# Own views for routed rows' stores, one table set for the first attention's roots, and an earlier first expert

## The chip, the cores and the metric

The kernel runs on one core of a Trainium2 chip. The core has five engines with a queue of instructions each: TensorE (PE, matrix products; PEld is its load of weights), VectorE (DVE), ScalarE (ACT, functions from tables, of which one set at a time is loaded), GpSimd (POOL) and SyncE (SP, which mostly issues DMAs). An engine works through its queue in order, and waits at an instruction until the semaphores that it needs are set. DMAs are issued by SP, ACT and POOL. The metric is device time in microseconds (us); lower is better.

## The reference

Two rounds of attention and of a mixture of experts (MoE) over x, 4 batches of 512 rows of 256 floats, and a context of 4 x 1601 rows of 256:

```
def _layernorm(x, axis=-1, eps=1e-05):
    m = jnp.mean(x, axis=axis, keepdims=True)
    v = jnp.var(x, axis=axis, keepdims=True)
    return (x - m) / jnp.sqrt(v + eps)
...
def _L0_xattn_ref(x, latents, ...):       # x: context, latents: layernorm of the rows
    xn = _layernorm(x, gamma_media, beta_media)
    ln = _layernorm(latents, gamma_lat, beta_lat)
    q = ln @ Wq + bq
    kv_input = jnp.concatenate([xn, ln], axis=1)
    k, v = jnp.split(kv_input @ Wkv + bkv, 2, axis=-1)
    ...
    attn = jax.nn.softmax(sim, axis=-1)   # 8 heads of 128, 512 x 2113 for each batch and head
    ...
    return out @ Wo + bo
...
x = x + _L0_xattn_ref(ctx_1024, _layernorm(x), ...)
x = x + _L0_ffn_ref(_layernorm(x), ...)   # top 2 of 8 experts, with a capacity, 256-1024-256, gelu
x = x + _L1_xattn_ref(ctx_1024, _layernorm(x), Wq, Wk, Wv, 1, 0, 1)   # 8 heads of 32, 512 x 1601
x = x + _L1_ffn_ref(_layernorm(x), ...)   # top 2 of 8 experts, softmax of the two, gelu
```

All of it is in float32.

## The kernel before

**Opening (0 to about 44 us).** For batch 0 `keys_input` (lines near L750 to L850) normalises the latents (`latents`, `latents_again`: two layer norms, one on the other), turns them with PE into `kvin`, and does the same with 13 tiles of context: `first` takes mean and variance of 4, 4 and 5 tiles with DVE's bn_stats and bn_aggr (L826, L827), the reciprocal root with `ln_scale`, and normalises on ACT (L834); `ctx_group` turns and scales. `queries_keys` makes qT and kT. All this is inside `in_order(computing)`: the engines run it in the order in which it is written, which is the list at L1024.

**Roots.** `ln_root` (L157) has two ways. While `both_tables` is set, by `logarithms(True)` (L128), it is Ln and Exp on ACT out of a table set that holds both. Otherwise it is Sqrt (L166), from another set than the attention's Exp (L958), and a reciprocal on DVE (L169). `ln_scale` adds one Newton step on DVE. `logarithms(True)` stands ahead of the second attention only.

**First attention (to about 1566 us).** A step n of the 128 is a batch b, a head h and a tile t of 128 rows. `scores` (PE, L944) fills the one buffer `ps_s`, 2113 columns; `top` (DVE, L952) takes the row maxima; `softmax` (ACT, L958) takes the exps into one of two `attn`; `exchange` (L965) sends 16 DMAs, 12 on SP and 4 on ACT, that swap blocks between partitions; `turn` (DVE, L973) ends the transpose into pT. For every two steps follow `weigh` (PE, L981), a copy oT (ACT, L1133) and `project` (PE, L992), whose result DVE adds to x (L1002). Work of the next heads and batches (queries, keys L890, values L927, moments) is laid between the steps in the list `later`, and a scheduler orders the instructions inside a step.

The main loop (L1053) runs four steps past the last, for the tail. At n == n_steps it closes the pool stack `right`, which holds what the attention needs on that side, opens the MoE's pools in its place, and calls `fetched(0, 0)` (L630: SP's loads of an expert's rows sx and weights w1, w2) and `turned` (L641: four transposes tp_x on PE, a copy sxT on DVE, L647). One step later comes `hidden` (L652: PE L657 and Gelu on ACT, L664), whose Gelus are kept in program order.

**First MoE (about 1566 to 1856 us).** Eight experts in two halves each: `fetched`, `turned`, `hidden` and the second layer (L1348, ps_y). Rows were scattered to experts' slots by POOL.

**Second attention (about 1856 to 2412 us).** 112 units of work and a tail of five, by a schedule that is written out (`place`, `put`), in order on PE, DVE and ACT. At a batch's end, on PE the result is turned (L1626), DVE divides it (`got`, L1636), and POOL adds it to x (L1643). Then `route2(b)` of that batch runs within the next batch's steps: layer norm, router, places of each row in its experts' lists, and `scatters` (L588): POOL's indirect DMAs store a row's 265 floats (`pay`: the normalised row and its number) in two DRAM tensors. For batches 0 to 2 that are eight scatters into `rows_a` (the experts' first tiles) and eight into `rows_b` (what overflows), for batch 3 eight into `rows_b`. They come out in pairs, between the other steps. Each scatter names the whole of `rows_a` or `rows_b` as its target (L594), so that the framework's tracker sees a write behind a write and makes it wait for the one before.

POOL's queue around the end of the second attention is, before and after the change: eight rows_a scatters of batch 2, an x-add (L1643), eight rows_b scatters, the last x-add (L1643), then the second MoE's stores. On DVE the layer norm of batch 3's last rows (L144, L145) and behind it the copy of the first expert's xT (L1487) follow that last x-add. SP's queue has `cw<-rows_a` (L1683, `load_first_rows`: the first expert's rows), then the loads of the next experts' rows (L1835) and weights (L1843).

**Second MoE (about 2404 to 2707 us).** `first_layer` (L1690) and `first_tile`: PE turns the rows (L1486), first layer (L1495), second (L1872); DVE scales y (L1899), POOL adds it to the output in DRAM by an indirect DMA (L1885). Overflowing rows are gathered from `rows_b` by POOL (L2009).

Of the kernel before, what the change touches and what calls it, by code (L numbers as in the profile page):

```python
# [7 lines left out]

F32 = mybir.dt.float32
# [66 lines left out]
def rows_of(i, n, tail):  # L76
    return tail if i == n - 1 else P
# [6 lines left out]
def xattn_ffn_twice(ctx: ExitStack, tc: tile.TileContext, a: dict, out: bass.AP):  # L84
# [355 lines left out]
    def route2(b, two, psum, tag, first=0, n=NT):  # L440
# [146 lines left out]
        def scatters():  # L587

            sent = 0
            for rows, at in ((rows_a, place_a), (rows_b, place_b))[b == B - 1 :]:  # L590
                for k in range(2):
                    for t in range(n):
                        j = b * NT + first + t
                        nc.gpsimd.indirect_dma_start(  # L594
                            out=rows[:, :],
                            out_offset=bass.IndirectOffsetOnAxis(ap=at[k][:, j : j + 1], axis=0),
                            in_=pay[:, t, :],
                            in_offset=None,
                            bounds_check=E * G - 1 if rows is rows_a else ROWS - 1,
                            oob_is_err=False,  # L600
                        )
                        sent += 1
                        if sent % 2 == 0:
                            yield
# [16 lines left out]
        yield from sending  # L621


    banks, tags = {}, {}

    def slots(of, e, half, n=CT):
# [46 lines left out]
    with ExitStack() as st:  # L673
# [72 lines left out]
        def keys_input(b, ctx_b):  # L746
# [68 lines left out]
            def ctx_group(n0):  # L815
                group(ctx_b, n0, min(4, NM - n0), S + n0 * P, gbm, TAIL, NM)

            def first(n0, n):
# [12 lines left out]
                for i in range(n):  # L831
                    r = rows_of(n0 + i, NM, TAIL)
                    of = ctx_b[:r, n0 + i, :]
                    nc.scalar.activation(  # L834
                        of, of, AF.Identity, scale=rs[:r, i : i + 1], bias=away[:r, i : i + 1]
                    )

            if b == 0:
                steps = [latents, latents_again, lambda: group(state["lat"], 0, NT, 0, gbl, P, NT)]

                groups = ((0, 4), (4, 4), (8, NM - 8))
                return steps, (
                    [lambda n0=n0, n=n: first(n0, n) for n0, n in groups],
                    [lambda n0=n0: ctx_group(n0) for n0 in range(0, NM, 4)],
                )

# [159 lines left out]
        def output_bias():  # L1006
# [8 lines left out]
            nc.vector.tensor_tensor(bo, bo, ps, ALU.add)  # L1015
            add_output_bias(0)

        opening = ExitStack()
        opening.enter_context(in_order(*computing))
        latent, context = keys_input(0, ctx_b)  # L1020
# [31 lines left out]
        early = late = ()  # L1052
        for n in range(n_steps + 4):  # L1053
            b, h, t = n // (H0 * NT), n // NT % H0, n % NT
            if n == n_steps:

                right.close()
                b_y = ctx.enter_context(tc.tile_pool(name="b_y", bufs=2, side="right"))
                b_two = ffn1.enter_context(tc.tile_pool(name="b_two", bufs=2, side="right"))
                banks.update(m=ps_t, h=ps_t)  # L1060
                tags.update(m="t", h="t")
                ahead = turned(*fetched(0, 0))
            if n == n_steps + 1:
                ahead = hidden(*ahead, behind=True)
            if n < n_steps:
                if t == 0:
# [1148 lines left out]
```

## Time and profile before

| | us |
|---|---|
| three runs | 2706.76, 2707.55, 2708.15 |
| their median | 2707.55 |
| the profiled execution | 2708.6 |
| its span, first to last instruction | 2706.9 |
| PE busy in it | 2634.4 |
| last matmul ends | 2693.2 |
| granted TensorE clock, mean over the span | 0.994 |
| one table load on ACT (35 of them) | 1.283 |
| scatters L594 into rows_a, rows_b | 24 and 32 |

Busy time is that of one profiled execution. An engine's wait is put down to the instruction that ended it. `x8` behind a row is the number of instructions that it stands for; one float32 matmul of L657, L944, L981 or L1348 shows as two of them. A granted clock of 1.00 means that TensorE's clock was let through whole.

### The profile page before, as it was taken

What the parts mean: (1) busy time and instruction counts of PE and PEld (TensorE: products, weight loads), DVE (VectorE), ACT (ScalarE), POOL (GpSimd) and SP (SyncE); (2) the same over time, 40 slices, a digit from 0 to 9 for tenths busy, and PEclk for the clock granted to TensorE, in tenths of its full rate; (3) what the DMA queues carried; (4) which work ended last, traced back from release to release, by engine and by line L of the source; (5) the groups of instructions that cost most, each with busy time, mean ns of one, the idle gap of its engine ahead of it and who ended that gap; (6) DMA issues with size and microseconds to landing.
All of it is one profiled execution on the core that took longest, in us unless ns stands there. A gap on an engine that the chain in (4) does not pass through costs nothing. (4 is left out here: it accounts for less than half of the span.)

```text
span 2706.9 us, 38439 instructions
## 1 busy us (share of the span) xinstructions
PE 2634.4 (97%) x14748; PEld 1790.0 (66%) x14748; DVE 1346.0 (50%) x2445; ACT 918.7 (34%) x1577; POOL 352.3 (13%) x372
## 2 busy tenths in 40 slices
PE   6999999999999999999999999999999999989997
PEld 3666676666666666766666678876454544458887
DVE  6544556644456544454454341124777878733111
ACT  4332234323334333333232321122444444452221
POOL 0000000100000100000100000102432431222542
PEclk9999999999999999999999999999999999999999
DMA  5444434433443433433343465553433200035673
GB/s 179 111 113 122 99 90 114 102 95 88 109 113 85 115 96 87 99 93 88 100 100 96 124 188 164 179 177 100 128 115 108 82 10 10 17 109 170 199 226 78
DMA packets 191325, 302.92 MB, mean 112 GB/s; under 512 B 41783, under 2 KB 113272, under 8 KB 188440
## 3 DMA queue, kind: packets, MB, share of 16 engines
q1 hardware_dynamic: 152392, 218.33, 28.9%
q0 software_dynamic: 14160, 46.31, 5.8%
q10 hardware_dynamic: 24576, 35.68, 5.2%
q8 instruction: 119, 1.95, 0.3%
q14 instruction: 78, 0.64, 0.1%
HBM read 111.46 MB, written 51.07 MB: 60 GB/s over the span
## 5 line engine op out<-in xcount | busy, mean ns | idle before, releaser
L952 DVE TENSOR_REDUCE top<-ps_s 128x1 f32<-128x2113 f32 x128 | 301.8, 2358 | 584.8 <-PE ps_s L944 583.6
L981 PE MATMUL ps_o<-pT,v 128*128 128x256 f32 x2176 | 519.4, 380 | 0.0
L944 PE MATMUL ps_s<-kT,qT 128*128 128x512 f32 (+1 forms) x1280 | 489.1, 526 | 5.8 <-ACT attn L958 5.8
L981 PEld LDWEIGHTS ps_o<-pT,v 128*128 128x128 f32 x2176 | 407.8, 190 | 110.6 <-issue 65.4
L958 ACT ACTIVATE attn<-ps_s,top 128x2113 f32<-128x2113 f32 x128 | 259.1, 2024 | 477.4 <-DVE top L952 457.8
L944 PEld LDWEIGHTS ps_s<-kT,qT 128*128 128x128 f32 x1280 | 241.8, 190 | 251.7 <-issue 235.8
L973 DVE STREAM_TRANSPOSE pT<-swapped 128x2176 f32<-128x2176 f32 x128 | 312.4, 2440 | 31.2 <-DMA swapped<-attn 22.5
L1295 DVE TENSOR_REDUCE tops<-ps_s 128x1 f32<-128x512 f32 (+2 forms) x428 | 251.5, 648 | 129.1 <-PE ps_s L1284 128.0
L890 PE MATMUL ps_k<-kvin,wkv 128*128 128x512 f32 (+2 forms) x640 | 259.4, 528 | 3.4 <-DVE kvin L810 3.0
L927 PE MATMUL ps_v<-wkv,kvin 128*128 128x256 f32 x1088 | 255.3, 381 | 2.0 <-ACT v L934 1.4
L927 PEld LDWEIGHTS ps_v<-wkv,kvin 128*128 128x128 f32 x1088 | 204.7, 190 | 38.4 <-issue 6.0
L1565 ACT ACTIVATE pT<-ps_w 128x512 f32<-128x512 f32 (+1 forms) x384 | 184.3, 565 | 124.5 <-PE ps_w L1551 124.4
L906 ACT ACTIVATE kT<-ps_k,bqk 128x512 f32<-128x512 f32 (+1 forms) x192 | 101.0, 556 | 259.9 <-PE ps_k L890 124.0
L890 PEld LDWEIGHTS ps_k<-kvin,wkv 128*128 128x128 f32 x640 | 115.7, 191 | 75.2 <-issue 64.0
L934 ACT COPY v<-ps_v 128x512 f32<-128x512 f32 x144 | 80.2, 561 | 213.1 <-PE ps_v L927 141.1
L1284 PE MATMUL ps_s<-kv,qT 32*128 32x512 f32 (+1 forms) x1024 | 127.7, 553 | 3.4 <-DVE got L1636 3.2
L1551 PE MATMUL ps_w<-qT,kv 32*128 32x256 f32 (+1 forms) x1664 | 118.0, 383 | 0.0
L657 PE MATMUL ps_h<-sxT,w 128*128 128x256 f32 (+1 forms) x512 | 108.0, 367 | 4.0 <-DVE sxT L647 2.5
L744 POOL TENSOR_TENSOR x<-x,bo 128x256 f32<-128x256 f32 x16 | 11.7, 760 | 742.9 <-DVE lat L182 545.6
L1348 PE MATMUL ps_y<-w,hT 128*128 128x256 f32 x480 | 107.8, 380 | 0.0
L657 PEld LDWEIGHTS ps_h<-sxT,w 128*128 128x128 f32 x512 | 91.8, 190 | 21.1 <-issue 4.2
L1348 PEld LDWEIGHTS ps_y<-w,hT 128*128 128x128 f32 x480 | 90.2, 190 | 14.9 <-issue 2.4
(317 smaller groups left out, 2764.3 us busy)
## 6 DMA issues: line engine op xcount, KB each, us to landing
swapped<-attn SPq DMA_DIRECT2D x1536, 68.0 KB
swapped<-attn ACTq DMA_DIRECT2D x512, 68.0 KB
w<-in_w_dram SPq DMA_DIRECT2D x32, 1024.0 KB
rows_b<-empty SPq DMA_DIRECT2D x36, 530.0 KB
w_e<-in_wall_dram SPq DMA_DIRECT2D x5, 2052.0 KB
cw<-in_ctxT_dram SPq DMA_DIRECT2D x4, 1601.0 KB
ctx_b<-in_ctx_dram SPq DMA_DIRECT2D x3, 1536.0 KB
slot_x<-scrap SPq DMA_DIRECT2D x8, 512.0 KB
```

The source lines that it names most:

```text
L657: nc.tensor.matmul(ps[:, f, :], lhsT=w1[:, c, (f0 + f) * P : (f0 + f + 1) * P], rhs=sxT[:, c, :], start=c == 0, stop=c == DC - 1,)
L890: nc.tensor.matmul(ps[:, :n], lhsT=wkv[:, c, hs], rhs=kvin[:, c, : n // 32, k, :] if k < 4 else flat_kvin[c][:, left : left + P], start=c ...
L927: nc.tensor.matmul(ps[:, k, :], lhsT=flat_kvin[c][:, j * P : (j + 1) * P], rhs=wkv[:, c, cols], start=c == 0, stop=c == DC - 1,)
L944: nc.tensor.matmul(flat[:, j0 : j0 + n], lhsT=qT[:, t * P : (t + 1) * P], rhs=kT[:, j0 : j0 + n], start=True, stop=True,)
L952: nc.vector.tensor_reduce(top, flat[:, :L], AX.X, ALU.max, negate=True)
L958: nc.scalar.activation(attn[:, :L], flat[:, :L], AF.Exp, bias=top, accum_out=total)
L973: nc.vector.transpose(pT[:, :, k * P : (k + 1) * P].rearrange("p c (a i) -> p a c i", a=4), swapped.rearrange("p a (c i) -> p a c i", i=32),)
L981: nc.tensor.matmul(ps, lhsT=v[:, j - parts[part][0], (h % 2) * DH0 : (h % 2 + 1) * DH0], rhs=pT[:, j, :], start=j == 0, stop=j == NB - 1,)
L1284: nc.tensor.matmul(pss[i][:, at : at + n], lhsT=qTs[b][rows, o, q0 : q0 + P], rhs=kvs[b][0][o][rows, j0 : j0 + n], start=True, stop=True,)
L1295: nc.vector.tensor_reduce(tops[u][:, t : t + at // n, some, j0 // 512], of, AX.X, ALU.max,)
L1348: nc.tensor.matmul(ps[:, t, :], lhsT=hT[:, f, t * P : (t + 1) * P], rhs=w2[:, f, :], start=f == 0, stop=f == FC - 1,)
L1565: nc.scalar.activation(pT[:r, i, :n], pss[2 * h + i][:r, :n], AF.Exp)
```

## The change

Three parts.

1. `dram_disjoint_views` makes eight views of `rows_a` and eight of `rows_b`, each over the whole tensor, which the framework takes as not overlapping with each other; a scatter of a batch writes through its own. Against the tensor itself (its first filling, and the loads from it) a view is ordered as before. The same view comes back at the next batch.
2. `logarithms(True)` now stands ahead of the opening and `logarithms(False)` at n == n_steps - 1. All roots of the first attention are thereby an Ln and an Exp on ACT; the table set is loaded once at the start, and the loads between Sqrt and Exp go. The moments of the opening's first four context tiles move from DVE to ACT: two activations with a running sum for each tile (`sums_of`), one giving minus the mean, one the sum of squared deviations, written over an attention buffer that is not yet in use. The first tile's stand between the latents' two roots, the others behind the second. The roots, Newton step and normalisation of these tiles are `first_of_sums` and `move`.
3. The block that stood at n == n_steps (closing `right`, the MoE's pools, `fetched`, `turned`) comes at n_steps - 1, and `hidden` of the first expert at n_steps instead of n_steps + 1.

In the order of instructions: SP's queue and POOL's are the same up to one small swap each in the MoE stages. PE has the same matmuls; its order differs at the end of the first attention, where tp_x (four transposes) now stands ahead of the last scores, the first expert's first layer lies around the second-last `weigh`, and its second layer (16 matmuls) wholly ahead of the last `weigh`. On DVE the copy sxT stands ahead of the last top. On ACT the last exp and its four DMAs still stand ahead of the first Gelu. In the opening ACT's order is: table load, Ln and Exp of the latents' first norm, two sums of tile 0, Ln and Exp of the second norm, six sums, a part of the latents' kvin, Ln and Exp of the four tiles, four normalisations.

```diff
+from concourse.ap import dram_disjoint_views
...
+                        rows_of_one = apart[rows is rows_b][k * n + t]
                         nc.gpsimd.indirect_dma_start(
-                            out=rows[:, :],
+                            out=rows_of_one[:, :],
...
+    apart = [dram_disjoint_views(rows[:, :], 2 * NT) for rows in (rows_a, rows_b)]
...
+            def sums_of(i):
+
+                if not sums:
+                    for name in ("less", "squares"):
+                        sums[name] = two.tile([P, 4], F32, tag=name, name=name)
+                of, to = ctx_b[:, i, :], attns[0][:, :D]
+                less, squares = (sums[k][:, i : i + 1] for k in ("less", "squares"))
+                nc.scalar.activation(to, of, AF.Identity, scale=-1.0 / D, accum_out=less)
+                nc.scalar.activation(to, of, AF.Square, bias=less, accum_out=squares)
+
+            def first_of_sums():
+
+                ve = two.tile([P, 4], F32, tag="ve4", name="ve")
+                nc.vector.tensor_scalar(ve, sums["squares"], 1.0 / D, EPS, ALU.mult, ALU.add)
+                _, rs = ln_scale(two, None, 4, ln_root(two, None, 4, ve))
+                away = two.tile([P, 4], F32, tag="nt4", name="away")
+                nc.vector.tensor_tensor(away, sums["less"], rs, ALU.mult)
+                move(0, 4, rs, away)
+
+            def move(n0, n, rs, away):
+                for i in range(n):
+                    r = rows_of(n0 + i, NM, TAIL)
+                    of = ctx_b[:r, n0 + i, :]
+                    nc.scalar.activation(
+                        of, of, AF.Identity, scale=rs[:r, i : i + 1], bias=away[:r, i : i + 1]
+                    )
...
-                steps = [latents, latents_again, lambda: group(state["lat"], 0, NT, 0, gbl, P, NT)]
-
-                groups = ((0, 4), (4, 4), (8, NM - 8))
+                steps = [
+                    latents,
+                    lambda: sums_of(0),
+                    latents_again,
+                    lambda: [sums_of(i) for i in range(1, 4)],
+                    lambda: group(state["lat"], 0, NT, 0, gbl, P, NT),
+                ]
+
+                groups = ((4, 4), (8, NM - 8))
                 return steps, (
-                    [lambda n0=n0, n=n: first(n0, n) for n0, n in groups],
+                    [first_of_sums] + [lambda n0=n0, n=n: first(n0, n) for n0, n in groups],
...
+        logarithms(True)
         opening = ExitStack()
...
-            if n == n_steps:
-
+            if n == n_steps - 1:
+
+                logarithms(False)
                 right.close()
                 b_y = ctx.enter_context(tc.tile_pool(name="b_y", bufs=2, side="right"))
                 b_two = ffn1.enter_context(tc.tile_pool(name="b_two", bufs=2, side="right"))
                 banks.update(m=ps_t, h=ps_t)
                 tags.update(m="t", h="t")
                 ahead = turned(*fetched(0, 0))
-            if n == n_steps + 1:
+            if n == n_steps:
                 ahead = hidden(*ahead, behind=True)
```

More of the change, by code (lines that the diff above doesn't have):

```diff
@@ L816, in ctx_group @@
                 group(ctx_b, n0, min(4, NM - n0), S + n0 * P, gbm, TAIL, NM)
+            sums = {}
+            def sums_of(i):
[20 more added lines that the diff above has]
+                    )
             def first(n0, n):
@@ L830, in first @@
                 nc.vector.scalar_tensor_tensor(away, mv[:, :, 0], -1.0, rs, ALU.mult, ALU.mult)
[L831 to L836, printed above, removed]
-            if b == 0:
-                steps = [latents, latents_again, lambda: group(state["lat"], 0, NT, 0, gbl, P, NT)]
-                groups = ((0, 4), (4, 4), (8, NM - 8))
+                move(n0, n, rs, away)
+            if b == 0:
+                steps = [
[6 more added lines that the diff above has]
+                groups = ((4, 4), (8, NM - 8))
                 return steps, (
-                    [lambda n0=n0, n=n: first(n0, n) for n0, n in groups],
+                    [first_of_sums] + [lambda n0=n0, n=n: first(n0, n) for n0, n in groups],
                     [lambda n0=n0: ctx_group(n0) for n0 in range(0, NM, 4)],
```

## The prediction

> **What bounds the kernel now.** I read the page first, then a table of the span cut into its stages, then the list of what TensorE waited for, then the order of time around the longest pauses. The page says that TensorE (PE) sets the time: it is busy in all but 72.5 us of the span.
>
> ```profile
> span 2706.9 us, 38439 instructions
> PE 2634.4 (97%) x14748; PEld 1790.0 (66%) x14748; DVE 1346.0 (50%) x2445; ACT 918.7 (34%) x1577; POOL 352.3 (13%) x372
> ```
>
> No matmul is added or taken away by the change, so all that can be won is pauses of PE and time at a lower clock. The table by stage (columns: stretch, its length, then busy time of PE, PEld, DVE, ACT, POOL, the granted clock, the DMA share, GB/s) shows where these are: the opening, the start and the end of the first attention, and the end of the second.
>
> ```profile
> 0.00:45.00 45.00, 26.10 (x74) 12.38 (x75) 23.82 (x119) 16.29 (x34) 1.73 (x12) 0.92 0.69 220
> 45.00:110.00 65.00, 60.88 (x208) 38.57 (x207) 42.11 (x90) 32.01 (x41) 0.00 (x0) 0.97 0.41 101
> 110.00:1540.00 1430.00, 1427.42 (x5359) 970.96 (x5358) 725.90 (x863) 465.75 (x664) 44.41 (x52) 1.00 0.41 100
> 1540.00:1640.00 100.00, 93.03 (x411) 71.96 (x410) 43.61 (x93) 25.44 (x35) 5.94 (x15) 1.00 0.58 178
> 2395.00:2425.00 30.00, 19.36 (x167) 14.25 (x167) 4.59 (x26) 9.97 (x20) 10.27 (x11) 0.89 0.32 98
> ```
>
> The waits (engine, its line, what ended the wait, us in total, times, longest) name them. The first line of this list is the opening's wait for the latents, 11.8 us, which nothing in the change shortens.
>
> ```profile
> PE ps_h L1495 <- DVE mv L145: 7.6, 1, 7.6
> PE ps_s L944 <- ACT attn L958: 5.8, 5, 2.1
> PE ps_h L657 <- DVE sxT L647: 2.5, 1, 2.5
> PE tp_f L1486 <- DMA cw<-rows_a: 2.0, 2, 1.9
> PE ps_h L657 <- ACT hT L664: 1.5, 1, 1.5
> POOL rows_b L594 <- DMA rows_b<-pay,place_b: 56.9, 25, 7.3
> POOL rows_a L594 <- DMA rows_a<-pay,place_a: 42.1, 18, 7.4
> ```
>
> **Separate views for the stores: the end of the second attention.** In order of time (start, length, engine, line, operation; idle time before it in brackets):
>
> ```profile
> 2395.56 0.98 POOL L594 DMA_INDIRECT rows_a<-pay,place_a  x1 [1.39 <-DMA rows_a<-pay,place_a]
> 2396.56 0.74 POOL L1643 TENSOR_TENSOR x<-x,got 128x256 f32<-128x256 f32 x1
> 2418.00 0.97 POOL L594 DMA_INDIRECT rows_b<-pay,place_b  x1 [1.74 <-DMA rows_b<-pay,place_b]
> 2418.99 0.74 POOL L1643 TENSOR_TENSOR x<-x,got 128x256 f32<-128x256 f32 x1
> 2420.84 0.75 DVE L144 BATCH_NORM_STATS2 st<-x 128x6 f32<-128x256 f32 x2 [7.81 <-DMA rows_b<-pay,place_b]
> 2422.36 8.67 PE L1495 MATMUL ps_h<-xT,w_kv 128*128 128x256 f32 x32 [7.56 <-DVE mv L145]
> ```
>
> POOL sends batch 2's 16 scatters one at a time, each behind the landing of the one before: the eight of rows_a run from 2374.72 to 2396.54, the eight of rows_b from 2397.47 to 2418.97. Behind them in POOL's order stands the last x-add, whose input got (L1636) is done at 2412.61. DVE's in-order bn_stats waits for that add, behind it stands the copy of xT, and PE waits for xT. So PE's 7.56 us are POOL's waits at L594, three engines on.
>
> With a view to each scatter the order of POOL around this point stays, while the wait for the neighbour goes; what is left is that a scatter waits for the one eight places ahead. All indices of the batch are ready on DVE at 2376.4, so eight scatters at 0.98 us plus some 0.1 between them end at about 2374.7 + 8 x 1.1 = 2383.5 and land about 2 us later (the bracketed waits were 1.4 to 2.1). The next x-add takes its got (done at 2389.34) at once, rows_b goes out from 2390.1 to about 2399, and POOL then sits ready for the last got. Three gains follow. (1) The load of cw from rows_a, which SP issued at 2397.73, goes out some 11 us sooner: PE's 1.89 us before tp_f go. (2) The last got comes at 2412.6 - 1.9 = 2410.7, the add (0.74) ends at 2411.5, bn_stats and the copy of xT take 1.42 (2420.84 to 2422.26) and end at 2413.0; PE's filler before it ends at 2414.8 - 1.9 = 2412.9. I leave 0.2 of the 7.56: a gain of 7.3. (3) The 32 matmuls at 2422.36 took 8.67 us against 7.17 for the same 32 at 2404.15; the granted clock is half from 2418.63 to 2425.45. Without the pause this and a few neighbours gain 1.6. Sum 10.8. Bounds: if the half clock stays and half of the pause too, 1.9 + 3.7 = 5.6; if xT comes with no wait at all, 11.1.
>
> What is late next? SP's loads for the following experts stand behind the landing of these same scatters: the third expert's weights go out at 2421.59 and are used at 2439.71, 18.1 us later. SP's gate is then the last add, near 2412, and PE's use 10.8 us sooner, near 2429: about 17 us apart, so covered. The earlier batches' scatters and batch 3's (2465 to 2499) lie beside PE work without a pause; their gain is put at 0, within 1 us either way, since 14 small pauses of the stretch 1860 to 2395 hang on DVE's maxima and on got.
>
> **One table set in the first attention.** A table load is 1.283 us. From 443 us on, ACT waits 457.8 us in all for the maxima (L952), and the step times of batches with a load equal those without: worth 0, and if that cover were gone 1.28 each. The first three exps have no cover:
>
> ```profile
> 46.03 1.28 ACT L958 ACT_TABLE_LOAD   x1 [5.99 <-DVE top L952]
> 55.87 1.28 ACT L958 ACT_TABLE_LOAD   x1
> 59.33 5.57 PE L944 MATMUL ps_s<-kT,qT 128*128 128x512 f32 x10 [2.15 <-ACT attn L958]
> 70.78 1.12 PE L944 MATMUL ps_s<-kT,qT 128*128 128x512 f32 x2 [0.65 <-ACT attn L958]
> ```
>
> Scores wait for the exp ahead, as one buffer holds them. The pauses are 0.84 (at 48.65), 2.15 and 0.65. A load less in front of each exp takes min(pause, 1.28): 0.84 + 1.28 + 0.65 = 2.8. The scores at 59.33 took 5.57 against 3.87 elsewhere, as the granted clock is half from 60.02 to 63.43; that pause shrinks to 0.87, and I take the 1.7 as won too. Bounds: 0 to 4.5. The extra Ln (0.21) and Exp (0.21) in place of a root (0.20) and a DVE reciprocal (0.18) change nothing in the chains of the opening.
>
> The Trainium skill, "ScalarE: Activation LUTs", section "What ACT_TABLE_LOAD costs", gives a switch 1283 ns plus a drain of about 1380 ns, 2.66 us together. Here the exp starts at 47.33 after a load from 46.03, with 0.02 us between; by the page each exposed switch would be worth up to 2.66, and the three pauses would go whole, 3.6 instead of 2.8. The trace decides.
>
> **Moments of the first four context tiles on ACT.** DVE loses four bn_stats and bn_aggr (13.91 to 16.1); ACT gets eight activations. Nearest row: L834, four in 2.07, 0.52 each; with the 0.19 that an accumulator read takes (L958), 0.71. The first two lie between the latents' two roots (7.94 and 9.79), the other six from about 10.2 to 13.3 or 14.5; the latents' turn on ACT starts at 14.03. So 0 to 0.5 us of delay there, while the tiles' normalisation starts at about 16.9 instead of 17.80. PE's pauses behind it (1.40 at 22.02, 2.62 at 25.94) hang on the second and third group as well. I take a gain of 0.3; bounds a loss of 0.9 and a gain of 0.9.
>
> **End of the first attention one step sooner.** PE's order gets tp_x of expert 0 ahead of the last scores, where it paused 1.09 us for the exp anyway (1561.15), and the copy of sxT ahead of the last top. That ends the 2.47 at L657; top(127) is later by at most the copy's 0.68. ACT still has the exchange's four DMAs (to 1574.8) and then the Gelu's load (1.28) ahead of the first Gelu, so this is done at about 1576.6; PE has until then 16 matmuls of the first layer (3.6) and 26 of the weighing (5.8), after a new wait of about 1.1 for DVE's transpose at 1569.3 to 1571.7. The second weighing needs the last step's exchange; SP's issue of it ends at 1583.0 as before, and PE now covers the time with expert 0's whole second layer (7.2 us). By my count PE ends that weighing near 1599.3 (before 1599.61) with five matmul pairs of 0.45 more behind it: a gain of 2.5. The queue ahead of SP's loads for expert 1 is the same, so these aren't sooner; they are needed from 1599 on, 15 us after issue. Bounds: a loss of 1 (a second wait for the exchange) and a gain of 4.0 (both pauses whole).
>
> **Sum**: 10.8 + 2.8 + 1.7 + 0.3 + 2.5 = 18.1, against the profiled execution's 2708.6 (span 2706.9 and 1.7 around it): 2690.5. The median of the runs shown, 2707.55, is 1.05 below that execution, so runs should give about 2689.5. PE has no pause from 2431 to its last matmul, so nothing there takes the gain up, and the tail of 13.7 us behind that matmul moves along.
>
> **Rivals.**
> B: the opening and the first attention's end give nothing, since PE only finds the same late data at its next pause (kvin at 28.56, the router behind batch 3's last rows at 1607). For: those two chains are not in the change. Against: from 71 to 1328 us PE never pauses, so what is won before stays won. 2707.55 - 10.8 = 2696.8.
> C: the 10.8 us at the end of the second attention come back as a wait for expert weights. For: the DMA engines are about 93% busy from 2425 to 2435. Against: the 17 us above. 2707.55 - 7.3 = 2700.3.
> D: the views change nothing in the waits (the landing of one scatter still holds the next). Against: the listed order of the changed program shows no such wait. Same 2700.3, but told apart by the L594 waits; with B or C on top 2705 to 2707, the case of no change.
> E, the other side: PE's clock. Two spells at half clock (2162.63 and 2224.07, 3.41 us each) came with no pause over 0.5 us in the 10 us ahead of them, so a denser PE may get more of them. Each costs 3.41 / 2 = 1.7 us. To end slower than before by 5.4 us, the 16.4 of the other terms and 5.4 have to be used up: 13 more spells, 2715 with 14. Against: 1430 us at 99.8% busy show a clock of 1.00.
>
> The Trainium skill, "TensorE: Matmul & The Clock Gate", section "Part 1: The HAM clock gate (the "warmup" mystery)", says that an idle window of about 3.4 us halves the clock. By it the 2.15 us pause should not have cost a spell, and removing it wins 1.7 less; the half clock from 60.02 stands right behind that pause, so I follow the row.
>
> **How the numbers follow.** A 0.57, B 0.15, C 0.10, D 0.05, two of B, C and D together 0.05, E 0.08. The time is A's, 2689.5. A's own range by its bounds is 2685 to 2695. Reaching to B and to the edge of C and D gives 2685 to 2700, which leaves out E, the doubled case and a part of C. What a measurement can tell from no change is 0.2%, 5.4 us. Faster: A, B, C, D = 0.87; same 0.05; slower 0.08.
>
> **What would show it.** L594's waits down from 99 us to some tens; PE at the first ps_h after the second attention with a pause under 1 us and a clock near 1 in 2395 to 2425; no table loads at L958 after the first exp, and the three pauses there summing to under 1.5; no pause over 1.5 us from 1555 to 1600. I am wrong if a new pause over 3 us appears behind 2410, if the ps_h of the first layer at 1570 waits for the transpose much longer than 1.1, or if the opening's first scores come later.

## The result, and the profile after

| | before | after |
|---|---|---|
| median of the runs, us | 2707.85 (4 runs, 2706.76 to 2711.1) | 2724.49 (4 runs, 2722.94 to 2725.79) |
| profiled execution, us | 2708.6 | 2722.94 |
| its span, us | 2706.9 | 2721.2 |
| granted clock, mean | 0.994 | 0.991 |

The changed kernel takes 1.0055 times as long, 95% interval 1.0043 to 1.0067: 16.6 us slower, where 18 us of gain were forecast. The page of the changed kernel says that PE's busy time grew by 21.1 us over the same 14,748 matmuls, while DVE, ACT and POOL do no more than before:

```profile
span 2721.2 us, 38428 instructions
PE 2655.5 (98%) x14748; PEld 1796.3 (66%) x14748; DVE 1341.3 (49%) x2420; ACT 899.0 (33%) x1589; POOL 352.5 (13%) x372
```

The list of waits of the changed kernel (engine, its line, what ended the wait, us in total, times, longest) has what was forecast and something new:

```profile
PE ps_o L1641 <- issue: 4.6, 8, 1.0
PE ps_o L1622 <- issue: 3.4, 6, 0.8
PE ps_s L977 <- ACT attn L991: 2.6, 3, 1.1
PE ps_h L660 <- DVE x L1035: 0.6, 1, 0.6
...
POOL rows_b L596 <- issue: 9.6, 32, 0.3
ACT sum L1600 <- remote: 7.7, 1, 7.7
ACT kv L1227 <- remote: 6.9, 1, 6.9
ACT pT L1600 <- remote: 6.5, 4, 4.5
POOL rows_a L596 <- issue: 5.7, 20, 0.3
DVE tops L1330 <- remote: 4.4, 1, 4.4
```

The old entries are gone: PE's 7.6 us ahead of the first ps_h, its 2.0 us ahead of tp_f, and POOL's 99 us behind its own scatters (L594 before, L596 now), which have become 0.3 us of issue each. New are waits of PE that nothing releases ("issue") and waits of ACT and DVE for which the profile finds no releaser on the core ("remote"). The kernel before has no wait of PE of the first kind on these lines, and none of the second.

What stands behind "remote" can be read from the semaphores. In the changed kernel, e2, e3, e13 and e14 each such wait from 1856 us on ended with an update of the one semaphore that PE's matmuls raise. The update came 1.7 to 6.6 us behind the modelled end of the last matmul that raises it, against 0.04 us in the median; that is too late for the profile to put the two together. So ACT and DVE waited for PE there, and what is held is PE, or its signals.

To see where the time went I set the two lists of matmuls beside each other, instruction by instruction, and took the start after minus the start before:

| place (from 1533 on: us in the changed kernel) | after minus before, us |
|---|---|
| first scores (42.8 against 43.6) | -0.8 |
| after the first head of batch 0 | -5.8 |
| 1533 | -6.8 |
| 1856 to 1863, start of the second attention | -10.0 to -10.6 |
| 2140 | -8.6 |
| 2180 | +0.4 |
| 2300 | +2.0 |
| 2330 | +9.0 |
| 2390 | +12.3 |
| 2410 | +20.0 |
| 2424 | +25.8 |
| end | +14.6 |

So everything up to the second attention is won, 36 us are lost within it, most of them between 2140 and 2424, and 11 us come back at its end. The loss lies in short stretches. This is the order of time in one of them, PE and then POOL of the changed kernel (start, length, engine, line, operation, idle time before it):

```profile
2168.43 1.23 PE L1586 MATMUL ps_w<-qT,kv 32*128 32x256 f32 x16
2169.59 0.91 PE L1622 MATMUL ps_o<-pT,kv 128*32 128x256 f32 x7
2171.31 0.42 PE L1622 MATMUL ps_o<-pT,kv 128*32 128x256 f32 x2 [0.81 <-issue]
2172.04 0.38 PE L1622 MATMUL ps_o<-pT,kv 128*32 128x256 f32 x1 [0.31 <-issue]
2172.77 0.61 PE L1622 MATMUL ps_o<-pT,kv 128*32 128x256 f32 x3 [0.35 <-issue]
2174.17 0.64 PE L1622 MATMUL ps_o<-pT,kv 128*32 128x256 f32 x3 [0.80 <-issue]
2174.74 1.93 PE L1319 MATMUL ps_s<-kv,qT 32*128 32x512 f32 x7
...
2169.25 0.98 POOL L596 DMA_INDIRECT rows_b<-pay,place_b  x1 [0.30 <-issue]
2170.53 0.98 POOL L596 DMA_INDIRECT rows_b<-pay,place_b  x1 [0.30 <-issue]
2171.81 0.98 POOL L596 DMA_INDIRECT rows_b<-pay,place_b  x1 [0.30 <-issue]
```

Sixteen matmuls that take 1.07 us elsewhere take 5.2 here, a few at a time, restarting about 0.72 us or twice that apart. POOL meanwhile sends scatters 1.28 us apart, ten in an unbroken row from 2159.6 on, and PE runs freely again when the row is over. The other long stretches lie on such rows too: 2315 to 2320 on one from 2304.8 to 2318.3, 2386.4 to 2396 on one from 2383.7 to 2393.8, 2416 to 2423 on one from 2410.3 to 2420.7. But a row alone is not enough. Eight indexed loads of POOL 1.32 us apart (1725.2 to 1735.5) and a row of nine stores beside the second MoE (2479.9 to 2491.8) cost nothing in the same trace. ACT waits through the stretches. In the one from 2386.4 it stands still for 7.71 us and starts again only at 2395.26:

```profile
2395.26 2.06 ACT L1600 ACTIVATE sum<-ps_w 128x512 f32<-128x512 f32 x4 [7.71 <-remote]
```

By stage (stretch, length, busy time of PE, PEld, DVE, ACT and POOL with their instructions, granted clock, DMA share, GB/s), the changed kernel:

```profile
45.00:110.00 65.00, 63.66 (x225) 41.37 (x225) 42.09 (x88) 23.43 (x37) 0.00 (x0) 1.00 0.45 112
1533.00:1630.00 97.00, 93.81 (x414) 72.50 (x413) 43.82 (x94) 25.50 (x35) 5.94 (x15) 1.00 0.60 184
2140.00:2395.00 255.00, 240.01 (x2745) 118.58 (x2737) 174.44 (x414) 110.54 (x235) 59.13 (x63) 0.96 0.08 27
```

and the kernel before in the last of these stretches:

```profile
2140.00:2395.00 255.00, 248.22 (x3075) 128.44 (x3070) 186.28 (x442) 125.39 (x266) 65.49 (x66) 0.99 0.08 28
```

In the same 255 us 330 matmuls fewer got through. The DMA engines are 8% busy in both, so the transfers' volume is not what holds PE. The clock fell from 0.99 to 0.96: after has five spells at half clock between 2140 and 2424, which begin at 2151.06, 2174.95, 2277.35, 2318.31 and 2393.41 and last 27.3 us together, worth 13.7 us. Each of them begins in the last microsecond of a row of scatters or within 4 us behind it.

### The profile page after: what moved, and what is told of

It is laid out like the page before. It is cut to its first block, busy times and chain, and to the rows that moved or that the text cites. A ratio compares the mean times of both kernels' runs of the same rounds, so it can differ in the third digit from the quotient of the medians.

```text
span 2721.2 us, 38428 instructions
## 1 busy us (share of the span) xinstructions
PE 2655.5 (98%) x14748; PEld 1796.3 (66%) x14748; DVE 1341.3 (49%) x2420; ACT 899.0 (33%) x1589; POOL 352.5 (13%) x372
## 5 line engine op out<-in xcount | busy, mean ns | idle before, releaser
L991 ACT ACTIVATE attn<-ps_s,top 128x2113 f32<-128x2113 f32 x128 | 259.0, 2024 | 492.4 <-DVE top L985 484.8
L1586 PE MATMUL ps_w<-qT,kv 32*128 32x256 f32 (+1 forms) x1664 | 124.1, 390 | 0.8 <-issue 0.7
L1622 PE MATMUL ps_o<-pT,kv 128*32 128x256 f32 (+1 forms) x1408 | 103.0, 395 | 3.6 <-issue 3.4
```

What stands on the lines that cost most here:

```text
L991: nc.scalar.activation(attn[:, :L], flat[:, :L], AF.Exp, bias=top, accum_out=total)
L1586: nc.tensor.matmul(pss[i][:r, k * QH : (k + 1) * QH], lhsT=kvs[b][0][o][rows, j * P : j * P + r], rhs=qTs[b][rows, o, f * QH : (f + 1) * Q ...
```

## The experiments

Two theories stood at the start. S: unbroken rows of indexed stores hold up the engines. H: the clock (rival E of the prediction) does it, through a denser PE. Line numbers of the experiments are those of the changed kernel where not said otherwise. Each time stands beside that of the kernel before on the same chip.

| label | time, us (runs) | before beside it | ratio, 95% interval | chip |
|---|---|---|---|---|
| e1_no_views | 2701.84 (4) | 2712.33 | 0.9957, 0.9941 to 0.9974 | 11 |
| e2_views_only | 2736.13 (1) | 2712.33 | | 11 |
| e3_two_views | 2722.31 (1) | 2712.33 | | 11 |
| e4_x_on_dve | 2700.03 (5) | 2712.33 | 0.996, 0.9946 to 0.9974 | 11 |
| e5_spaced8 | 2718.76 (1) | 2707.62 | | 4 |
| e6_spaced4 | 2692.1 (1) | 2707.62 | | 4 |
| e7_plain | 2687.99 (1) | 2707.62 | | 4 |
| e8_spaced1 | 2687.37 (1) | 2710.99 | | 14 |
| e9_spaced2 | 2685.06 (4) | 2710.99 | 0.9905, 0.9888 to 0.9922 | 14 |
| e10_pairs | 2690.27 (1) | 2710.99 | | 14 |
| e11_tile_only | 2685.91 (1) | 2707.62 | | 14 |
| e12_fours | 2684.13 (1) | 2707.62 | | 14 |
| e13_after_again | 2729.06 (2) | 2709.05 | 1.0077, 1.0047 to 1.0106 | 15 |
| e14_tile_only_again | 2731.99 (3) | 2709.05 | 1.008, 1.005 to 1.011 | 15 |
| e15_after_third | 2687.0 (2) | 2711.95 | 0.9908, 0.9889 to 0.9928 | 1 |
| e16_spaced1_again | 2687.64 (2) | 2711.95 | 0.9911, 0.9891 to 0.9931 | 1 |
| e17_spaced2_again | 2685.15 (4) | 2711.95 | 0.9906, 0.9889 to 0.9922 | 1 |
| e18_spaced4_again | 2692.41 (4) | 2711.95 | 0.9926, 0.991 to 0.9943 | 1 |

### Which part of the change: e1 to e3

**e1, the change without the views.**

```diff
-                            out=rows_of_one[:, :],
+                            out=rows[:, :],
```

> The changed kernel with its scatters aimed at the whole tensors again; the table set, the moments on ACT and the earlier first expert stay. Theory (back-to-back scatters on POOL hold up the dense instruction streams of PE and ACT in the second attention, some 36 us): the time is that of before less what the other two parts win up to 1856 us, 10.0 to 10.6 us: about 2697.5; PE shows no pauses put down to issue between 2140 and 2425, and the 7.56 us pause ahead of the first ps_h of the second mixture is back. Rival (the other two parts, or a clock that is halved more often by a denser PE, cause the loss): 2715 or more, with the same late stretches in the second attention.

PE is 7.9 to 9.9 us ahead of the kernel before from 1856 to 2400. In the second attention it has no wait of the kind "issue", and no engine has one of the kind "remote". The old pause is back and has grown, since PE now comes earlier to the same late data (order of time, e1):

```profile
2413.41 0.75 DVE L145 BATCH_NORM_STATS2 st<-x 128x6 f32<-128x256 f32 x2 [10.08 <-DMA rows_b<-pay,place_b]
2414.92 9.91 PE L1530 MATMUL ps_h<-xT,w_kv 128*128 128x256 f32 x32 [9.83 <-DVE mv L146]
```

**e2, the views alone**, in the kernel before.

```diff
+from concourse.ap import dram_disjoint_views
...
+    apart = [dram_disjoint_views(rows[:, :], 2 * NT) for rows in (rows_a, rows_b)]
...
-                            out=rows[:, :],
+                            out=apart[rows is rows_b][k * n + t][:, :],
```

> The kernel before with the views alone. Theory (scatters back to back): 2707.9 + 36 - 11 = about 2733 (2728 to 2738), the late stretches lying on the bursts of POOL. Rival (loss from the other parts): 2697, as forecast for the views.

The matmuls are at -0.2 at 1875, +9.2 at 2180, +16.7 at 2330 and +37.0 at 2400; then some 9 come back. The new waits are there without the other two parts of the change (list of waits, e2):

```profile
ACT pT L1568 <- remote: 11.0, 5, 4.6
...
ACT kv L1195 <- remote: 7.0, 1, 7.0
DVE tops L1298 <- remote: 4.5, 1, 4.5
PE ps_o L1609 <- issue: 2.2, 3, 1.0
```

So the loss belongs to the views. A denser PE (H) does not bring it: in e1 PE is as dense, and nothing is lost until the old pause.

**e3, two views for each tensor in turn**, so that at most two scatters are under way.

```diff
-                        rows_of_one = apart[rows is rows_b][k * n + t]
+                        rows_of_one = apart[rows is rows_b][(k * n + t) % 2]
```

> The changed kernel with two views in turn instead of eight, so that a scatter waits for the landing of the one two places ahead: at most two under way, issued some 1.5 to 2 us apart instead of 1.28. If the cause is many scatters under way or issued without a break, the late stretches go or shrink to under 10 us in all: 2687 to 2697. If two under way are enough: about 2724, as with eight.

From 2160 on the late stretches are those of eight views: 31.5 us are lost in the second attention, against 36.5 in the changed kernel, and some 11 come back. The scatters of rows_b follow each other at the same 1.28 us, and at 1.41 to 1.43 beside the second MoE. So more than two under way are not needed. The run says no more about the number, as it hardly changes it: a store lands about 2 us behind its issue, so that at 1.28 us seldom more than two are under way with eight views either.

### The pause at the end: e4

**e4, e1 with batch 3's additions (L1678) on DVE.**

```diff
-            nc.gpsimd.tensor_tensor(
+            (nc.vector if b == B - 1 else nc.gpsimd).tensor_tensor(
```

> As e1_no_views, with batch 3's x-adds on DVE, which makes their input, instead of POOL behind the scatters. Theory (the 7.56 us pause is POOL's queue: the add stands behind scatters that wait for each other): PE's pause ahead of the first ps_h goes to under 0.5 us and the half clock behind it with it, 7.3 + 1.6 = 9 us less than e1: about 2688.5. Rival (DVE's statistics wait for the landing of the rows_b scatters themselves, as the label of the wait says, or SP's loads behind that landing come too late for the third expert): the time of e1, 2697.5, or a new pause of PE between 2415 and 2440.

The last addition is done on DVE at 2405.24, ahead of POOL's remaining scatters. The statistics still wait (order of time, e4):

```profile
2404.82 0.42 DVE L1678 TENSOR_TENSOR x<-x,got 128x256 f32<-128x256 f32 x1
...
2411.13 0.75 DVE L145 BATCH_NORM_STATS2 st<-x 128x6 f32<-128x256 f32 x2 [5.63 <-DMA rows_b<-pay,place_b]
```

PE's pause is 5.24 us, and the kernel is 1.8 us faster than e1, within the two intervals. The prediction put the 7.56 us down to the addition that stands behind the scatters on POOL. But DVE also waits for the landing of the last scatter itself, and that wait ends last: the statistics start 0.31 to 0.32 us behind it in the kernel before (landed at 2420.53, start 2420.84), in e1 (2413.09, 2413.41) and in e4 (2410.81, 2411.13), while the addition of the kernel before had ended at 2419.73. The prediction's own line for L144 names that landing. The views take both waits away, so the gain of the step came whole, with some luck: its chain had a wrong link.

### Is it the pace? e5 to e12

The next theory: what counts is the time between two scatters. e5, e6, e8 and e9 put k writes of a small tile behind each scatter on POOL, with k = 8, 4, 1 and 2; the scatters are then 3.37, 2.42, 1.34 and 1.96 us apart.

```diff
+                        rest = two.tile([P, 96], F32, tag="rest", name="rest")
+                        for _ in range(8):
+                            tc.keep_in_program_order(nc.gpsimd.memset(rest, 0.0))
```

> The changed kernel with its eight views, and eight small memsets on POOL behind each scatter: no scatter waits for another, but they are issued some 2.5 us apart instead of 1.28. Theory (stores issued without a break hold up the other engines): no late stretch between 2140 and 2425; the chain of 16 scatters takes about as long as the serial one, so the 7.56 us pause is partly or wholly back: 2695 to 2705. Rival (it is not the rate but that stores don't wait for each other at all, or the views themselves): 2718 or more.

> As e5_spaced8 with four memsets, some 1.9 us from scatter to scatter. Theory with a threshold between 1.28 and 2.4 us: if 1.9 us is slow enough, no late stretch and the last adds some 10 us sooner: about 2688; if not, late stretches of half the length or more: 2705 to 2715.

> One memset behind each scatter, by the rows of e6 some 1.77 us from scatter to scatter. If the other engines are held up whenever the next store is issued before the last has landed (2.4 us and more in the serial kernel): late stretches of some 15 us and more left, about 2700 to 2715. If what counts is the share of time that POOL spends in issuing, with a threshold below 55%: none, and the pause ahead of the second mixture under 1 us: about 2686.

> Two memsets, some 1.99 us from scatter to scatter (49% of POOL's time in issuing). If 1.99 us is slow enough: the chain of 16 takes 32 us instead of 38, the pause of 3.63 us that e6 had left goes and the half clock behind it: 2687 (2684 to 2690), the fastest so far. If not, late stretches beside the bursts: 2695 to 2710.

No late stretch in any of them. e5 is still 11 us slower than the kernel before, because it paces too slowly: sixteen scatters at 3.37 us are 54 us, and what stands behind them comes late (list of waits of PE, 1856 to 2440, e5):

```profile
PE ps_h L1533 <- DVE mv L146: 12.0, 1, 12.0
PE tp L196 <- POOL pay L459: 7.2, 5, 3.2
PE tp_f L1524 <- DMA cw<-rows_a: 3.9, 1, 3.9
```

e6 still has a pause of 3.6 us ahead of the first ps_h; e8 and e9 have none over 0.2 there. But e8, at 1.34 us hardly slower than the change's 1.28, should have shown late stretches by the theory of the pace.

**e7, plain stores:** in e1, the rows_b stores of batches 0 to 2 become plain DMAs of POOL into a scratch tensor, so that these rows are missing from rows_b.

```diff
+                        if rows is rows_b and b < B - 1:
+                            nc.gpsimd.dma_start(plain[(k * B * NT + j) * P : (k * B * NT + j + 1) * P, :], pay[:, t, :])
+                        else:
...
+    plain = dram.tile([2 * B * NT * P, PAY], F32, name="plain")
```

> As e1_no_views (scatters into the whole tensors, one behind the other), but the eight rows_b stores of each of batches 0 to 2 are plain DMAs issued by POOL, without indices, into parts of a scratch tensor of their own, that wait for nothing; so the overflow rows of these batches do not reach rows_b. If any DMAs issued by POOL back to back hold up the others: late stretches beside these bursts, 15 to 20 us, 2700 to 2707 with the 9.8 us pause gone. If only indexed stores do: none, about 2690.

They go out 0.55 us each, and there is neither a late stretch nor the pause.

e10 puts the eight writes behind every second scatter only, e12 one write after every fourth, e11 a single one ahead of a batch's scatters, which are then an unbroken row at 1.28 us as in the change:

```diff
+                        if sent == 0:
+                            rest = two.tile([P, 96], F32, tag="rest", name="rest")
+                            tc.keep_in_program_order(nc.gpsimd.memset(rest, 0.0))
```

> Eight memsets behind every second scatter: two scatters 1.28 us apart, then 3.4 us, on the mean 2.3 us as in e6 (2.43). If two stores under way at once are what holds up the others: late stretches in every pair, 2700 or more. If it is the mean rate, or a backlog that only a longer row of stores builds up: as e6, 2690 to 2693.

> The changed kernel with the small tile of e8 and one memset, ahead of a batch's first scatter only; the rows of scatters behind it stay unbroken, 1.28 us apart. If the late stretches come from unbroken rows of indexed stores: they are back, 2715 to 2727. If e8 was rid of them by the tile alone (it moves other tiles in the on-chip memory): none, about 2687.

> One memset behind every fourth scatter: rows of four. If any POOL instruction between them ends what builds up, and four are too short a row to do harm (the row of four at 2270 us in the changed kernel had half a microsecond): 2686 to 2692. If one memset per four is not enough: late stretches of 10 us and more, 2695 to 2715.

None of the three has a late stretch, e11 neither. Either the one write (or its tile) matters, or something outside the program. The runs up to here left that open: every kernel with late stretches had run on chip 11 or in the first comparison, and e5 to e12 on chips 4 and 14.

### The same program on other chips: e13 to e18

e13 is the changed kernel itself, e14 is e11 itself, on the same chip.

> The changed kernel as it is, on the same chip as the next one. If the late stretches belong to the program (the placing of its tiles among it): 2722 to 2727, late stretches as before. If they belong to some chips: on a chip without them about 2686.

> As e11_tile_only, beside e13_after_again on one chip. If the tile or its memset rids the program of the late stretches: 2684 to 2688 whatever the other shows. If it is the chip: as e13 shows, within 3 us.

Both lose: 2729.06 and 2731.99. The kernel that took 2685.91 as e11 takes 46 us more as e14, with the same waits as the changed kernel (list of waits, e14):

```profile
ACT pT L1603 <- remote: 11.6, 5, 4.6
ACT qT L1289 <- remote: 10.2, 1, 10.2
POOL rows_b L599 <- issue: 9.5, 32, 0.3
DVE tops L1333 <- remote: 9.4, 3, 4.6
```

So neither the write nor the tile had taken the late stretches away. The theories of the pace and of the tile lose their support with that: e5 to e12 ran where no late stretch was seen in any kernel, and say nothing about what would prevent one. That holds for e7 too: it does not show that plain stores would be free of them.

e15 is the changed kernel once more; e16 to e18 are e8, e9 and e6 again, all on one further chip.

> The changed kernel as it is, the control of the next three on one chip. On a chip like those of the first comparison, e2 and e13: 2722 to 2732, with late stretches. On a chip like that of e8 to e12: 2684 to 2688 without any, which by itself shows that the chip decides; the next three then come within 6 us of it.

> As e8, 1.34 us from scatter to scatter with a memset between. Where e15 has late stretches: as e15 (within 6 us) if the pace counts, 2690 or less if any instruction between two scatters is enough.

> As e9, 1.97 us from scatter to scatter. Where e15 has late stretches: 2685 to 2690 if 1.97 us is slow enough, 2695 to 2715 if not.

> As e6, 2.42 us from scatter to scatter, near the serial kernel's 2.4 to 3.1. Where e15 has late stretches: 2690 to 2694, none left (theory: the pace counts); 2700 or more if stores that do not wait for each other do harm at any pace.

Here the changed kernel takes 2687.0, 25 us less than the kernel before beside it. Its page has the instructions of the first comparison, and 25.9 us less of busy PE:

```profile
span 2685.1 us, 38428 instructions
PE 2629.6 (98%) x14748; PEld 1787.9 (67%) x14748; DVE 1340.5 (50%) x2420; ACT 898.8 (33%) x1589; POOL 351.4 (13%) x372
```

The order of time in the step that was shown above, and POOL's row over it (e15):

```profile
2165.10 1.03 PE L1586 MATMUL ps_w<-qT,kv 32*128 32x256 f32 x16
2166.06 1.07 PE L1622 MATMUL ps_o<-pT,kv 128*32 128x256 f32 x16
2167.06 1.14 PE L1319 MATMUL ps_s<-kv,qT 32*128 32x512 f32 x8
...
2165.15 0.97 POOL L596 DMA_INDIRECT rows_b<-pay,place_b  x1 [0.30 <-issue]
2166.43 0.98 POOL L596 DMA_INDIRECT rows_b<-pay,place_b  x1 [0.30 <-issue]
2167.71 0.97 POOL L596 DMA_INDIRECT rows_b<-pay,place_b  x1 [0.30 <-issue]
```

The same matmuls beside the same row of scatters at the same 1.28 us, and they take 1.07 us. PE has no wait of the kind "issue" over 0.2 us, ACT and DVE none of the kind "remote". By stage, the stretch of the losses and the end of the second attention (e15):

```profile
2140.00:2395.00 255.00, 248.20 (x3116) 130.48 (x3114) 180.04 (x428) 128.24 (x270) 68.22 (x73) 1.00 0.10 35
2395.00:2435.00 40.00, 38.80 (x202) 34.01 (x201) 15.78 (x91) 15.66 (x31) 5.51 (x4) 1.00 0.61 207
```

and the first ps_h behind it in order of time (e15):

```profile
2402.07 7.14 PE L1530 MATMUL ps_h<-xT,w_kv 128*128 128x256 f32 x32 [0.17 <-issue]
```

Between 2395 and 2435 the clock is whole; the pause ahead of the first ps_h is 0.17 us, and its 32 matmuls take 7.14.

**What is shown and what stays open.** Shown: the views, and no other part, bring the loss (e1 against e2 and e3 on one chip; e2 and e3 ran once each, 21.6 and 7.8 us above the slowest of eight runs of the kernel before). Shown too: the same program has it on some chips and not on others (the changed kernel 2724.49, 2729.06 and 2687.0; e11 and e14), while the kernel before takes 2707.6 to 2712.3 on all of them. No chip was seen in both conditions, so the chip itself and what it did at that time cannot be told apart. The late stretches lie on unbroken rows of scatters, and are absent where most stores wait for the one before (e1, e4: mostly 2.3 us and more apart, but for a few pairs at 1.28); that is a coincidence in time on several traces, and its mechanism is not shown.

The chips can be told apart by kernels that lose nothing, too. The table has the latest signal of PE (semaphore update behind the modelled end of its matmul, 1856 to 2440 us), and how many of the 3088 single landings of POOL's DMAs, 16 for each, the trace recorded:

| traces | latest signal, us | landings recorded |
|---|---|---|
| rows on chips 11 and 15 and in the first comparison (changed kernel, e2, e3, e13, e14) | 4.8 to 6.7 | 2158 to 2238 |
| no such rows, chip 11 and first comparison (kernel before, e1, e4) | 0.90 to 1.45 | 2685 to 2754 |
| chips 4, 14 and 1 (e5 to e12, e15 to e18) | 0.14 | 3029 to 3084 |

Of the 878 landings that the changed kernel's first trace lacks, 832 belong to DMAs of POOL with a neighbour 1.75 us away or less. This leaves a rival that no run tests. Each time on record belongs to an execution whose span and clock were recorded, and where the stretches appear the records have holes. So it is not excluded that the recording has a part in the loss.

Open: what in the chip, its state or the recording decides; why PE goes on in steps of about 0.72 us; why its signals come late; and whether stores held apart (e9, e17) would be free of the loss where the changed kernel shows it, since no paced kernel has run there. The volume of the stores does not explain the stretches: those of batch 0 into rows_b move 576 bytes each, some 460 bytes per us, and the stretch shown above lies on them. Nor does a late packet of PE's instructions show: the packets of 16 KB that the trace calls instruction packets come about every 9 to 15 us, and around the step shown above they start at 2163.61 and 2182.06, in e15 at 2160.88 and 2172.11, on either side of the step in both.

**Versions.** The fastest of those run more than once is the changed kernel with two small writes behind each scatter: 0.9906 (0.9889 to 0.9922) on one chip and 0.9905 (0.9888 to 0.9922) on another, though not distinguishable from the change itself on the first of these (0.9908, 0.9889 to 0.9928). Those that beat the kernel before on a chip with late stretches are without the views: e1, 0.9957 (0.9941 to 0.9974), and e4, 0.996 (0.9946 to 0.9974).

## Why the prediction was wrong, step by step

The priced terms came out near their sizes, though one chain had a wrong link (e4); a step that was put at nothing did not. On the chip without late stretches the steps can be read one by one (e15 against the profile before, both aligned as above):

| step | predicted gain, us | measured, us |
|---|---|---|
| moments on ACT, opening | 0.3 | 0.5 (first comparison: 0.8; 18 traces: a loss of 0.7 to a gain of 0.9) |
| three exps without a load, and the half clock | 2.8 + 1.7 | 5.0 |
| loads from 443 us on | 0 | 1.5 (first comparison: 1.0) |
| end of the first attention | 2.5 | 3.7 |
| the earlier batches' scatters | 0, within 1 | -0.1 (first comparison: a loss of 36.5) |
| end of the second attention | 10.8 | 11.2 (first comparison: 11) |
| sum | 18.1 | 21.8 (first comparison: a loss of 14.6) |

**The step that failed** is this sentence: "The earlier batches' scatters and batch 3's (2465 to 2499) lie beside PE work without a pause; their gain is put at 0, within 1 us either way". I asked only what a scatter that comes sooner would give, and not what its waits had kept apart. The 25 and 18 waits that the list showed for L594 were what held most scatters of a batch 2.3 us and more apart; without them they follow each other at 1.28. Their removal turns pairs into rows of up to ten, and with such a row beside a dense stretch of PE, ACT and DVE the trace of before had nothing to bound its cost. A price that no row bounds needed an open loss in the range; I gave it 1 us. The runs showed 36.5 us of loss in its place in the first comparison, about 42 in e13 and none in e15; why some chips show it stays open. The range was also too narrow by its own terms: the lower bounds add up to 5.6 + 0 - 0.9 - 1 = 3.7 and the upper to 11.1 + 4.5 + 0.9 + 4.0 = 20.5, which is 2687 to 2704 and not the 2685 to 2695 that it names. For batch 3, beside the second MoE, the step held: the distance between the kernels does not change after 2438, in the first comparison either.

**Opening.** ACT takes 0.42 + 0.19 and 0.51 + 0.19 for the two sums of a tile, 1.3 us a tile against my 1.42, and is through at 13.1, so that the latents' turn is not delayed; the four tiles' normalisation starts at 15.68 instead of 17.80, where I had 16.9. What that is worth cannot be told: in the 18 traces with this opening the first scores come between 0.9 us earlier and 0.7 us later than in the one trace of the kernel before.

**One table set.** Of the pauses 0.84, 2.15 and 0.65 there is one left, 0.86 us at 55.29, where the prediction had 0.87; the spell at half clock from 60.02 is gone, and the scores behind the pause take 3.87, as predicted. The larger price that the prediction names beside its own, by which the three pauses would go whole, does not hold here. In the list of waits the other two of the three for L991 lie at the end of the first attention (1.09 and 0.65).

The Trainium skill, "TensorE: Matmul & The Clock Gate", section "Part 1: The HAM clock gate (the "warmup" mystery)", counts on about 3.4 us of idle time for the clock to fall. The long pauses agree: in e1 PE stops at 2405.09 and the half clock comes at 2410.28. For the 2.15 us pause the runs side with the row that I followed: with 0.86 us left of it the spell is gone in the changed kernel, and in e2, which keeps the loads, it is there again (59.72).

**End of the first attention.** The pauses of 1.09, 2.47 and 1.51 us are gone. In their place stand 0.65 (for the exp), 0.59 (for DVE's addition, L1035) and 0.36 (for inv); the wait of 1.1 for DVE's transpose that I allowed does not appear. The last weighing runs from 1583.98 to 1591.3 instead of 1592.11 to 1599.6: the second layer that I laid ahead of it fits in full. Of these 8.1 us 6.8 had been won before, so the end that I put near 1599.3 compares with 1598.1. The term was 1.2 too small.

**End of the second attention.** tp_f's wait gave about 1.9, the pause 7.39 (7.56 to 0.17) and the half clock about 1.6 in the first comparison, against 1.9, 7.3 and 1.6. The weights of the third expert did not become a wait (rival C is wrong). The chain behind the 7.3 lacked the wait that e4 showed.

**Earlier batches in e15.** The -0.1 is a balance: e15 has a spell at half clock from 1927.24 to 1934.07 that costs 3.1 us, and lacks the two spells of the kernel before at 2162.63 and 2224.07.

**Rivals.** B is wrong: what was won early was still there at 2140. D is wrong: the waits at L596 are gone. E has the right side and the wrong cause. Its clock did fall in the second attention, but behind or in stretches in which PE got through little, and with the views; e1, with the same density, has two spells of 3.41 us before 2400, as many as the kernel before has between 64 and 2418.

## What to carry to other kernels

A wait may be what spaces a stream of transfers; before it is taken away, price the dense stream that is left, beside the engines that run then, and not only the waits. Where the profile has no such stream, the step is an unknown with a loss on its open side, whatever the sum says. When a change contradicts its trace-based sum, run the same program on another chip before looking for a cause in the program.

## What the runs showed of the hardware

- Rows of four to ten indexed stores of POOL, 1.28 us apart, coincide on some chips with stretches in which PE hardly advances and ACT and DVE wait for it: 36.5 us in the second attention in the first comparison, about 42 in e13. On other chips the same rows cost nothing (e15), and neither does the row beside the second MoE (2479.9 to 2491.8 in the changed kernel).
- Where these stretches appear, a signal of PE reaches the waiting engine up to 6.7 us behind the modelled end of its matmul (e14); on chips 4, 14 and 1 it is 0.14 us at most (1856 to 2440 us).
- The same program lies 42 us apart on two chips (2729.06 and 2687.0), while the kernel before differs by 3 between them (2709.05 and 2711.95).
- An indexed store occupies POOL for 0.98 us, a plain one for 0.55 (e7).
